# Last layer of a four-layer graph network: source blocks in pairs, count rows on four row groups, clamps shared by two engines in a fixed order

## Chip, cores and metric

One core of a Trainium2 chip runs one program. The metric is the device time of one execution in microseconds (us); the median of three runs is given. The core has five engines with a queue each, which they work through in order: TensorE (PE in the profile; its weight loads are PEld), VectorE (DVE), ScalarE (ACT), GpSimd (POOL) and SyncE (SP, which issues most transfers). Matmuls write to PSUM, eight banks of 128 x 512 float32.

## The reference, cut to what matters

Four graph layers on 4096 nodes with 64 features and one 0/1 adjacency matrix (about 32 edges a row). Each layer is applied to the ReLU of the normalized x and added to x. The change is in the last layer, with a little in the layer before it:

```python
def _L2_gnn_ref(X, adj, W, b):
    deg = jnp.clip(jnp.sum(adj, axis=1, keepdims=True) + 1.0, 1.0, None)
    h_neigh = (adj @ X + X) / deg
    z = jnp.concatenate([X, h_neigh], axis=1) @ W + b
    out = jax.nn.relu(z)
    return out / jnp.maximum(jnp.linalg.norm(out, axis=1, keepdims=True), 1e-12)

def _L3_gnn_ref(input, adj, weight, bias):
    support = input @ weight
    mask = (adj != 0).astype(support.dtype)
    rank = jnp.cumsum(mask, axis=1)
    deg = rank[:, -1:]
    k = jnp.minimum(deg, 100.0)
    pos = rank - (deg - k)
    w = mask * jnp.where(pos > 0, 0.5 ** (k - pos), 0.0)
    return w @ support + bias
```

So in the last layer an edge of a node weighs one half to the power of the number of the node's edges with a higher index, and only the last 100 edges count.

## The kernel before

Nodes are cut into 32 blocks of 128 (NB = 32, P = 128) and into 8 groups of 512 (G = 512, four blocks each). The adjacency lies transposed in memory: rows are sources, columns are targets. An earlier stage has written it to scratch memory as 8-bit masks (mask_d), whose byte is 1.0 in the fp8 format where there is an edge.

**Layer 2** (`layers_fast`, L2690 to L2738) runs over two halves of 2048 targets. For each half TensorE adds up all source blocks (nacc, L2701) and the edge counts (dc, L2711), and `layer2_group` (L2641) then finishes four groups, one after the other: fold (pnf, L2647), concatenation (cat, L2652 and L2653), two transposes, product with the weights (pz, L2658), ReLU and norm (zt and nrm, L2662 to L2671), addition to x (L2673), normalization (`norm_steps`, L964), and the support of the last layer (psup, L2681), split into a high and a low half in SS (L2684 to L2687). At the end of a half a matmul with a triangular matrix turns the counts of each source block into the counts of all later blocks (plate, L2737), and VectorE clamps them into the tile late (L2738): 128 rows are 4 groups of targets times 32 source blocks.

**The last layer** (L2741 to L2811) goes over four quarters u of 1024 targets (two groups of 512, NK = 2), and in each over the 32 source blocks j:

1. two count matmuls (L2767) with 32 contraction rows each: they pick the row of block j from late and write minus 128 times the number of edges in later blocks to every row of pv. They use the 32 rows that belong to the group of targets, so the two lie in different row groups of TensorE;
2. two edge matmuls (L2775) add, with the matrix tri, 100 x 128 for an edge of the row itself and minus 128 for each edge in a later row of the block. pv is two banks wide, and there are two of them;
3. ScalarE clamps pv at zero and writes 16-bit integers (L2784). Read as bfloat16, they are powers of two: the weights;
4. two adding matmuls (L2749) of the block before add up support times weights in sacc, two banks.

After 32 blocks ScalarE and VectorE copy sacc to ev (L2794), 16 small matmuls fold the high and the low half (pn, L2799), VectorE adds bias and x (L2807 and L2808), and GpSimd issues the transfer to the output (L2809).

VectorE has one more task: it checks that all entries of the adjacency are 0 or 1 (`count_odd`, L951 to L957; another program branch would otherwise compute the result). Each of 64 checks loads 1 MB of the float32 matrix (raw, two buffers) and takes one VectorE instruction. Sixteen of them belong to the last layer, none of them before the last support is ready (`issue_after(valued[-1].ins)`). The results are reduced after the layer (L2843 to L2846).

The order on each engine is set by a scheduler that builds the program; it may move an instruction ahead of others that were written earlier. Where code stands in `in_order` (L927), the instructions of TensorE, VectorE and ScalarE written there keep their order among themselves; others may come in between. Before the change the last layer isn't in such a block. A tile of a pool has as many buffers as `bufs` says, and an instruction that writes a buffer waits for the readers of its former content.

Of the kernel before, what the change touches and what calls it, by code (L numbers as in the profile page):

```python
# [24 lines left out]
P = 128  # L25
N = 4096
NB = N // P
D = 64
G = 512
NG = N // G  # L30
GB = G // P
# [804 lines left out]
def kernel(  # L836
# [111 lines left out]

        return col.unsqueeze(2).to_broadcast([P, col.shape[1], width])

    def count_odd(pool, c):  # L951

        raw = pool.tile([P, HW], F32, name="raw", tag="raw", bufs=2)
        nc.sync.dma_start(raw, adjT[c % NB * P : (c % NB + 1) * P, c // NB * HW : (c // NB + 1) * HW])
        nc.vector.scalar_tensor_tensor(  # L955
            raw, raw, 0.0, raw, ALU.is_gt, ALU.not_equal, accum_out=bad[:, c : c + 1]
        )  # L957
# [1576 lines left out]
    def layers_fast(es, wide, *sums):  # L2534
# [75 lines left out]
        with not_before_nodes():  # L2610
# [28 lines left out]
        late = lp.tile([P, 2, G], BF16, name="late")  # L2639

        def layer2_group(b0, part, deg):  # L2641

            bs = slice(b0, b0 + GB)
            hg = h[:, bs, :]
            pn = ps.tile([P, GB, D], F32, name="pnf", tag="misc")
            for b in range(GB):
                nc.tensor.matmul(  # L2647
                    pn[:, b, :], lhsT=part[:, b * P : (b + 1) * P], rhs=fold_h, start=True, stop=True
                )
            cat = work.tile([P, GB, 2 * D], F32, name="cat", tag="cat")  # L2650
            nc.gpsimd.tensor_copy(cat[:, :, 0:D], hg)
            nc.vector.scalar_tensor_tensor(cat[:, :, D:], pn, 1.0 / VALH, hg, ALU.mult, ALU.add)  # L2652
            nc.vector.tensor_tensor(cat[:, :, D:], cat[:, :, D:], over(deg, D), ALU.mult)  # L2653
            cT = work.tile([P, G], F32, name="cT", tag="cT")
            transpose_to(cT, [cat[:, b, :] for b in range(GB)], P, ps, nc.scalar.copy)
            pz = ps.tile([P, GB, D], F32, name="pz", tag="misc")
            for b in range(GB):
                nc.tensor.matmul(  # L2658
                    pz[:, b, :], lhsT=cT[:, b * P : (b + 1) * P], rhs=w2, start=True, stop=True
                )  # L2660
            zt = work.tile([P, GB, D], F32, name="zt", tag="zt")
            nc.vector.tensor_tensor(zt, pz, b2t.unsqueeze(1).to_broadcast([P, GB, D]), ALU.add)  # L2662
# [24 lines left out]
            nc.scalar.activation(SS[:, bs, 1, :], lo, AF.Copy, scale=LO)  # L2687


        with tc.tile_pool(name="ps_nacc", bufs=6, space=PSUM) as ps_acc:  # L2690
            for hf in range(2):
# [44 lines left out]
                pl = ps.tile([P, G], F32, name="plate", tag="misc")  # L2736
                nc.tensor.matmul(pl, lhsT=lat, rhs=cnt16[:, hf], start=True, stop=True)  # L2737
                nc.vector.tensor_scalar(late[:, hf], pl, VBITS, None, ALU.min)  # L2738


        ps_acc = es.enter_context(tc.tile_pool(name="ps_sacc", bufs=2, space=PSUM))  # L2741
        ps_v = es.enter_context(tc.tile_pool(name="ps_v", bufs=2, space=PSUM))
        for u in range(4):
            hs = slice((u % 2) * HO2, (u % 2 + 1) * HO2)
            accs = [ps_acc.tile([P, G], F32, name="sacc", tag="sacc") for _ in range(NK)]

            def add_up(j, w):
                for k in range(NK):
                    nc.tensor.matmul(  # L2749
                        accs[k],  # L2750
                        lhsT=SS[:, j].rearrange("p s d -> p (s d)"),
                        rhs=w[:, k * G : (k + 1) * G].bitcast(BF16),
                        start=(j == 0),
                        stop=(j == NB - 1),
                    )

            last = None
            for q in range(NQ):
                m = work.tile([P, JT, HO2], U8, name="m3", tag="m3", bufs=3)
                nc.sync.dma_start(m, mask_d[q][u // 2][:, :, hs])  # L2760
                for t in range(JT):
                    j = q * JT + t

                    pv = ps_v.tile([P, HO2], F32, name="pv", tag="pv")
                    for k in range(NK):
                        r = ((u % 2) * NK + k) * O
                        nc.tensor.matmul(  # L2767
                            pv[:, k * G : (k + 1) * G],
                            lhsT=blk[r : r + O, j, :],
                            rhs=late[r : r + O, u // 2, :],  # L2770
                            start=True,
                            stop=False,
                        )
                    for k in range(NK):
                        nc.tensor.matmul(  # L2775
                            pv[:, k * G : (k + 1) * G],
                            lhsT=tri,
                            rhs=m[:, t, k * G : (k + 1) * G].bitcast(F8),
                            start=False,
                            stop=True,  # L2780
                        )

                    w = work.tile([P, HO2], I16, name="w3b", tag="w3b", bufs=3)
                    nc.scalar.activation(w, pv, AF.Relu)  # L2784
                    if j % 8 == 4:
                        with tc.issue_after(valued[-1].ins):
                            count_odd(work, next(todo))
                    if last is not None:
                        add_up(*last)
                    last = (j, w)  # L2790
            add_up(*last)
            ev = work.tile([P, NK, G], F32, name="ev3", tag="ev3")
            for k in range(NK):
                (nc.vector.tensor_copy if k % 2 else nc.scalar.copy)(ev[:, k, :], accs[k])  # L2794
            for k in range(NK):
                b0 = (u * NK + k) * GB
                pn = ps.tile([P, GB, D], F32, name="pn3", tag="misc")
                for b in range(GB):
                    nc.tensor.matmul(  # L2799
                        pn[:, b, :],  # L2800
                        lhsT=ev[:, k, b * P : (b + 1) * P],
                        rhs=fold_3,
                        start=True,
                        stop=True,
                    )
                og = work.tile([P, GB, D], F32, name="og", tag="og")
                nc.vector.tensor_tensor(og, pn, b3t.unsqueeze(1).to_broadcast([P, GB, D]), ALU.add)  # L2807
                nc.vector.tensor_tensor(og, og, x[:, b0 : b0 + GB, :], ALU.add)  # L2808
                nc.gpsimd.dma_start(  # L2809
                    out[b0 * P : (b0 + GB) * P, :].rearrange("(b p) f -> p b f", p=P), og  # L2810
                )  # L2811
        assert next(todo, None) is None

    with tc.If(general == 0):
        with ExitStack() as es:
# [86 lines left out]
```

## Time and profile before

| | us |
|---|---|
| median of three runs (2017.6, 2022.05, 2024.63) | 2022.05 |
| the profiled execution | 2025.07 |
| its span, from the first to the last instruction | 2023.3 |
| TensorE matmul busy | 1805.3 (89%) |
| VectorE busy | 1539.6 (76%) |
| ScalarE busy | 1469.6 (73%) |
| GpSimd busy | 83.4 (4%) |
| first count matmul of the last layer, from the start of the span | 1811.7 |
| first edge matmul of its second quarter | 1880.2 |
| end of its last adding matmul | 2012.3 |

The profile is of one execution. A group's row gives line, engine, operation, output and inputs with shapes, the number of instructions, then busy time in us, the mean of one in ns, and the idle time of the engine just before them with what ended it. In the timeline a row gives start and length in us of instructions of one kind that follow each other; starts are counted from the start of the span. "L2775" is a line of the kernel before. Matmuls overlap: a 512-column matmul lasts 0.38 us in the rows, and the next one can start 0.22 us after it.

### The profile page before, as it was taken

What the parts mean: (1) busy time and instruction counts of PE and PEld (TensorE: products, weight loads), DVE (VectorE), ACT (ScalarE), POOL (GpSimd) and SP (SyncE); (2) the same over time, 40 slices, a digit from 0 to 9 for tenths busy, and PEclk for the clock granted to TensorE, in tenths of its full rate; (3) what the DMA queues carried; (4) which work ended last, traced back from release to release, by engine and by line L of the source; (5) the groups of instructions that cost most, each with busy time, mean ns of one, the idle gap of its engine ahead of it and who ended that gap; (6) DMA issues with size and microseconds to landing.
All of it is one profiled execution on the core that took longest, in us unless ns stands there. A gap on an engine that the chain in (4) does not pass through costs nothing. (4 is left out here: it accounts for less than half of the span.)

```text
span 2023.3 us, 44172 instructions
## 1 busy us (share of the span) xinstructions
PE 1805.3 (89%) x19323; PEld 816.2 (40%) x19340; DVE 1539.6 (76%) x2251; ACT 1469.6 (73%) x1427; POOL 83.4 (4%) x125
## 2 busy tenths in 40 slices
PE   5889999999999999997699958999999985889997
PEld 3444444444444444444244432333333333454332
DVE  5779988998789979996788768888878788533530
ACT  3768888899688878993889756777777743227676
POOL 2000100100000000001011000000000000000000
PEclk8989999999999999997799968999999997889999
DMA  8946565434211111103355415444344336312852
GB/s 111 179 116 101 100 101 72 166 123 161 96 49 49 49 49 54 54 2 93 127 178 181 154 59 188 141 145 155 121 144 150 116 119 221 125 63 74 290 188 65
DMA packets 117016, 239.05 MB, mean 118 GB/s; under 512 B 11062, under 2 KB 84006, under 8 KB 102054
## 3 DMA queue, kind: packets, MB, share of 16 engines
q1 hardware_dynamic: 101996, 192.95, 28.2%
q0 software_dynamic: 14816, 43.18, 12.0%
q8 instruction: 153, 2.51, 0.5%
q14 instruction: 51, 0.42, 0.1%
HBM read 245.37 MB, written 49.46 MB: 146 GB/s over the span
## 5 line engine op out<-in xcount | busy, mean ns | idle before, releaser
L1205 ACT ACTIVATE st<-srow,nt 128x2048 int8<-128x2048 f32 x352 | 682.6, 1994 | 84.6 <-DVE B L1211 83.7
L1211 DVE TENSOR_TENSOR B<-st,mres 128x1024 int32<-128x1024 int32 x256 | 311.8, 1220 | 64.7 <-PE accC L1541 39.8
L1541 PE MATMUL accB<-B,ybh 128*32 128x512 fp8e4 x3072 | 327.3, 384 | 13.0 <-DVE B L1211 13.0
L1541 PE MATMUL accD<-B,ybh 128*32 128x512 fp8e4 x2048 | 289.3, 387 | 1.6 <-DVE h L1674 1.6
L1541 PEld LDWEIGHTS <-ybh 128*32 128x32 bf16 (+1 forms) x6656 | 193.1, 98 | 213.3 <-issue 48.4
L1541 PE MATMUL accC<-B,ycn 128*32 128x512 fp8e4 x2272 | 267.9, 383 | 1.2 <-issue 1.2
L1541 PE MATMUL accC<-mres,ych 128*32 128x512 fp8e4 x2272 | 268.8, 384 | 0.0
L1541 PE MATMUL accL<-B,ybh 128*32 128x512 fp8e4 x1536 | 213.2, 386 | 3.4 <-DVE h L1673 3.4
L1541 PEld LDWEIGHTS <-ych 128*32 128x32 f16 x4096 | 164.5, 98 | 116.7 <-issue 9.4
L1199 DVE TENSOR_SCALAR st<-srow,nt 128x2048 uint8<-128x2048 f32 x160 | 205.1, 1284 | 2.1
L2352 PE MATMUL accj<-sg,who 128*64 128x512 f32 (+1 forms) x512 | 196.4, 614 | 6.9 <-DVE sg L2345 6.4
L2352 PE MATMUL acci<-sg,who 128*64 128x512 f32 (+1 forms) x512 | 196.5, 614 | 0.0
L2308 ACT ACTIVATE yt<-pu,consts 128x512 f32<-128x512 f32 x144 | 98.6, 686 | 99.7 <-PE pu L2307 99.6
L955 DVE SCALAR_TENSOR_TENSOR raw<-raw 128x2048 f32<-128x2048 f32 x64 | 146.0, 2284 | 31.4 <-DMA raw<-in_adj_dram 31.4
L2297 ACT ACTIVATE sg<-pl,rb 128x512 f32<-128x512 f32 x256 | 160.7, 678 | 7.9 <-PE pl L2292 4.7
L2784 ACT ACTIVATE w3b<-pv 128x1024 int16<-128x1024 f32 x128 | 130.9, 1023 | 42.6 <-PE pv L2775 41.1
L1205 ACT ACTIVATE st<-srowo,nto 128x1024 int8<-128x1024 f32 x128 | 138.0, 1136 | 14.8 <-DVE B L1211 12.4
L1541 PE MATMUL accC<-C,ych 128*32 128x512 fp8e4 x1824 | 143.0, 385 | 2.1 <-DVE C L1219 2.1
L1219 DVE TENSOR_TENSOR C<-B,mres 128x1024 int32<-128x1024 int32 x114 | 139.6, 1225 | 3.8 <-PE accC L1541 0.6
L1541 PEld LDWEIGHTS <-ycn 128*32 128x32 f16 x2272 | 105.9, 98 | 65.0 <-issue 5.3
L2345 DVE SCALAR_TENSOR_TENSOR sg<-pf,sg 128x512 f32<-128x512 f32 x112 | 72.1, 685 | 38.6 <-PE pf L2342 38.6
L2286 PE MATMUL pl<-nm,noid 128*128 128x512 fp8e4 x256 | 82.3, 393 | 14.3 <-ACT sg L2297 13.4
(498 smaller groups left out, 2678.8 us busy)
## 6 DMA issues: line engine op xcount, KB each, us to landing
raw<-in_adj_dram SPq DMA_DIRECT2D x64, 1024.0 KB, 5.8
mo<-edges SPq DMA_DIRECT2D x32, 512.0 KB, 3.9
noedge<-nmo POOLq DMA_DIRECT2D x32, 512.0 KB, 3.8
nm<-noedge SPq DMA_DIRECT2D x64, 256.0 KB, 3.1
m<-edges SPq DMA_DIRECT2D x16, 1024.0 KB, 4.7
m<-edges SPq DMA_DIRECT2D x32, 512.0 KB, 4.1
srow<-srow_d SPq DMA_DIRECT2D x15, 1024.0 KB, 6.8
mres<-in_adj_dram POOLq DMA_DIRECT2D x8, 1024.0 KB, 36.0
```

What stands on the lines that cost most here:

```text
L955: nc.vector.scalar_tensor_tensor(raw, raw, 0.0, raw, ALU.is_gt, ALU.not_equal, accum_out=bad[:, c : c + 1])
L1199: nc.vector.tensor_scalar(st[:, i, :].bitcast(U8), srow, negs[:, i : i + 1], EDGE, ALU.is_gt, ALU.mult)
L1205: nc.scalar.activation(st[:, i, :], srow, AF.Sign, bias=negs[:, i : i + 1], scale=-1.0)
L1211: nc.vector.tensor_tensor(B.bitcast(I32), st.bitcast(I32), edges.bitcast(I32), ALU.bitwise_and)
L1219: nc.vector.tensor_tensor(C.bitcast(I32), B.bitcast(I32), edges.bitcast(I32), ALU.bitwise_xor)
L1541: ins = nc.tensor.matmul(acc[k * O : (k + 1) * O, :], lhsT=values, rhs=moving(k), start=start, stop=stop,)
L2286: nc.tensor.matmul(pl, lhsT=noid, rhs=nm[:, b, :].bitcast(F8), start=True, stop=False)
L2297: nc.scalar.activation(sg[:, b0 + k, :], pl, AF.Sigmoid, bias=rb[:, j : j + 1], scale=1.0)
L2308: nc.scalar.activation(far[gi, gj][:, b, :], pu, AF.Sigmoid, bias=nb_t, scale=2.0 * DIST_K / (DIST_S * DIST_S),)
L2345: nc.vector.scalar_tensor_tensor(v[:, t, :], pf, F_K3, v[:, t, :], ALU.add, ALU.mult)
L2352: nc.tensor.matmul(acc[r : r + n, :], lhsT=XQ[:, src, cols], rhs=w, start=start, stop=stop)
L2784: nc.scalar.activation(w, pv, AF.Relu)
```

## The change

The last layer goes over pairs of source blocks: n counts 64 pairs, 16 in each quarter.

- A pair has four pv tiles of one bank each (before: two blocks in flight, of two banks each). Its four count matmuls come first, then its four edge matmuls. The second block's count rows are read from late_x, a second copy of late with its upper and lower 64 rows exchanged, so that the four matmuls use four different row groups. VectorE writes late_x with two more instructions a half.
- The clamp is done in pieces of 512: VectorE takes the first group of both blocks, ScalarE the second. In every fourth pair (n % 4 == 2) ScalarE takes all four, and VectorE checks 1 MB of the adjacency instead. The load of the next check's rows is issued right after a check. The checks are no longer held back until the last support is ready, so four of the sixteen are in the first quarter.
- The adding matmuls (four) of the pair before follow. The folds of a quarter are deferred: the last adding matmuls of a quarter stand in the first pair of the next, the copies to ev behind them, and the fold matmuls and the output in the pair after that.
- Everything stands in `in_order`.
- The bias is added to x by GpSimd in layer 2, behind the normalization, so that one VectorE operation remains for the output; its transfer is issued by SP. The reduction of the check results stands ahead of the last adding matmuls. In the built program the two operations that follow it also stand ahead of the last copy to ev on VectorE, and GpSimd has two more library reloads, one ahead of the first bias addition and one ahead of the all-partition reduction.

Line numbers after the change are 7 to 33 higher: L2762 is the count matmul, L2770 the edge matmul, L2784 and L2786 the clamps of ScalarE and VectorE, L2794 the adding matmul, L2805 the copy to ev, L2814 the fold, L2821 the output addition, L962 the check.

```diff
+    def load_rows(pool, c):
         raw = pool.tile([P, HW], F32, name="raw", tag="raw", bufs=2)
         nc.sync.dma_start(raw, adjT[c % NB * P : (c % NB + 1) * P, c // NB * HW : (c // NB + 1) * HW])
+        return raw, c
+
+    def count_odd(pool, c):
+        check_rows(*load_rows(pool, c))
+
+    def check_rows(raw, c):
         nc.vector.scalar_tensor_tensor(
...
+            nc.gpsimd.tensor_tensor(xg, xg, b3t.unsqueeze(1).to_broadcast([P, GB, D]), ALU.add)
...
                 nc.vector.tensor_scalar(late[:, hf], pl, VBITS, None, ALU.min)
+                for lo, hi in ((slice(0, D), slice(D, P)), (slice(D, P), slice(0, D))):
+                    nc.vector.tensor_scalar(late_x[lo, hf], pl[hi], VBITS, None, ALU.min)
 
         ps_acc = es.enter_context(tc.tile_pool(name="ps_sacc", bufs=2, space=PSUM))
-        ps_v = es.enter_context(tc.tile_pool(name="ps_v", bufs=2, space=PSUM))
-        for u in range(4):
...
+        ps_v = es.enter_context(tc.tile_pool(name="ps_v", bufs=4, space=PSUM))
+        PAIRS = NB // 2
+        rows = load_rows(work, next(todo))
+        edges, accs, last, ready = None, {}, None, None
+        both = [(i, k) for i in range(2) for k in range(NK)]
+
+        def ranks(u, j0):
+            pvs = {ik: ps_v.tile([P, G], F32, name="pv", tag="pv") for ik in both}
+            for i, k in both:
+                r = ((u + i) % 2 * NK + k) * O
+                nc.tensor.matmul(
+                    pvs[i, k],
+                    lhsT=blk[r : r + O, j0 + i, :],
+                    rhs=(late, late_x)[i][r : r + O, u // 2, :],
+                    start=True,
+                    stop=False,
+                )
+            for i, k in both:
+                nc.tensor.matmul(
+                    pvs[i, k],
+                    lhsT=tri,
+                    rhs=edges[:, j0 % JT + i, k * G : (k + 1) * G].bitcast(F8),
+                    start=False,
+                    stop=True,
+                )
+            return pvs
+
+        def clamp(pvs, alone):
+            w = work.tile([P, 2, HO2], I16, name="w3b", tag="w3b")
+            for i, k in both:
+                wk = w[:, i, k * G : (k + 1) * G]
+                if k or alone:
+                    nc.scalar.activation(wk, pvs[i, k], AF.Relu)
+                else:
+                    nc.vector.tensor_scalar(wk, pvs[i, k], 0.0, None, ALU.max)
+            return w
+
+        def add_up(u, j0, w):
+            if j0 == 0:
+                accs[u] = [ps_acc.tile([P, G], F32, name="sacc", tag="sacc") for _ in range(NK)]
+            for i, j in enumerate(range(j0, j0 + 2)):
...
+            if j0 + 2 < NB:
+                return None
             ev = work.tile([P, NK, G], F32, name="ev3", tag="ev3")
-            for k in range(NK):
-                (nc.vector.tensor_copy if k % 2 else nc.scalar.copy)(ev[:, k, :], accs[k])
+            for k, acc in enumerate(accs.pop(u)):
+                (nc.vector.tensor_copy if k else nc.scalar.copy)(ev[:, k, :], acc)
+            return u, ev
+
+        def bring(u, ev):
             for k in range(NK):
...
-                nc.vector.tensor_tensor(og, pn, b3t.unsqueeze(1).to_broadcast([P, GB, D]), ALU.add)
-                nc.vector.tensor_tensor(og, og, x[:, b0 : b0 + GB, :], ALU.add)
-                nc.gpsimd.dma_start(
+                nc.vector.tensor_tensor(og, pn, x[:, b0 : b0 + GB, :], ALU.add)
+                nc.sync.dma_start(
...
+        with in_order():
+            for n in range(4 * PAIRS):
+                u, j0 = n // PAIRS, n % PAIRS * 2
+                if j0 % JT == 0:
+                    q, c = j0 // JT, u % 2 * HO2
+                    edges = work.tile([P, JT, HO2], U8, name="m3", tag="m3", bufs=3)
+                    nc.sync.dma_start(edges, mask_d[q][u // 2][:, :, c : c + HO2])
+                pvs = ranks(u, j0)
+                w = clamp(pvs, n % 4 == 2)
+                if n % 4 == 2:
+                    check_rows(*rows)
+                    rows = (next(todo, None),)
+                    if rows[0] is not None:
+                        rows = load_rows(work, rows[0])
+                done = add_up(*last) if last else None
+                if ready:
+                    bring(*ready)
+                ready, last = done, (u, j0, w)
+            nc.vector.tensor_reduce(bad[:, 0:1], bad, AX.X, ALU.add)
+            bring(*add_up(*last))
...
-        nc.vector.tensor_reduce(bad[:, 0:1], bad, AX.X, ALU.add)
         odd = spool.tile([P, 1], F32, name="odd")
```

More of the change, by code (lines that the diff above doesn't have):

```diff
@@ L949, in over @@
         return col.unsqueeze(2).to_broadcast([P, col.shape[1], width])
-    def count_odd(pool, c):
+    def load_rows(pool, c):
         raw = pool.tile([P, HW], F32, name="raw", tag="raw", bufs=2)
         nc.sync.dma_start(raw, adjT[c % NB * P : (c % NB + 1) * P, c // NB * HW : (c // NB + 1) * HW])
+        return raw, c
+    def count_odd(pool, c):
+        check_rows(*load_rows(pool, c))
+    def check_rows(raw, c):
         nc.vector.scalar_tensor_tensor(
@@ L2638, in layers_fast @@
             nc.vector.tensor_scalar(fold_3, fold_h, M3, 2.0**27 / VAL, ALU.mult, ALU.mult)
-        late = lp.tile([P, 2, G], BF16, name="late")
+        late, late_x = (lp.tile([P, 2, G], BF16, name=n) for n in ("late", "late_x"))
         def layer2_group(b0, part, deg):
@@ L2738, in layers_fast @@
                 nc.vector.tensor_scalar(late[:, hf], pl, VBITS, None, ALU.min)
+                for lo, hi in ((slice(0, D), slice(D, P)), (slice(D, P), slice(0, D))):
+                    nc.vector.tensor_scalar(late_x[lo, hf], pl[hi], VBITS, None, ALU.min)
         ps_acc = es.enter_context(tc.tile_pool(name="ps_sacc", bufs=2, space=PSUM))
-        ps_v = es.enter_context(tc.tile_pool(name="ps_v", bufs=2, space=PSUM))
-        for u in range(4):
-            hs = slice((u % 2) * HO2, (u % 2 + 1) * HO2)
-            accs = [ps_acc.tile([P, G], F32, name="sacc", tag="sacc") for _ in range(NK)]
-            def add_up(j, w):
+        ps_v = es.enter_context(tc.tile_pool(name="ps_v", bufs=4, space=PSUM))
@@ L2748, in add_up @@
                 for k in range(NK):
                     nc.tensor.matmul(
-                        accs[k],
+                        accs[u][k],
                         lhsT=SS[:, j].rearrange("p s d -> p (s d)"),
-                        rhs=w[:, k * G : (k + 1) * G].bitcast(BF16),
+                        rhs=w[:, i, k * G : (k + 1) * G].bitcast(BF16),
                         start=(j == 0),
@@ L2755, in add_up @@
                     )
[L2757 to L2764, printed above, removed]
-                    for k in range(NK):
[L2766 to L2791, printed above, removed]
+            if j0 + 2 < NB:
+                return None
             ev = work.tile([P, NK, G], F32, name="ev3", tag="ev3")
-            for k in range(NK):
-                (nc.vector.tensor_copy if k % 2 else nc.scalar.copy)(ev[:, k, :], accs[k])
+            for k, acc in enumerate(accs.pop(u)):
+                (nc.vector.tensor_copy if k else nc.scalar.copy)(ev[:, k, :], acc)
+            return u, ev
+        def bring(u, ev):
             for k in range(NK):
```

## Prediction, made before the changed kernel ran

> **What bounds it now.** I read the slices first: after 1810 us TensorE is at nine tenths or more in nearly every slice, ScalarE and VectorE are not. The table of windows then splits the last layer into the quarter that overlaps with the tail of layer 2 (1811.7 to 1880), the other three quarters, and the end. Columns: length, then busy time and count of PE, PEld, DVE, ACT, POOL, then granted clock, DMA share, GB/s.
>
> ```profile
> 1811.70:1880.00 68.30, 64.17 (x322) 29.73 (x328) 25.88 (x66) 46.38 (x70) 0.80 (x2) 0.93 0.21 64
> 1880.00:2012.30 132.30, 129.55 (x609) 43.76 (x618) 39.24 (x47) 98.64 (x99) 4.95 (x7) 1.00 0.58 200
> 2012.30:2023.30 11.00, 2.02 (x17) 1.86 (x16) 2.21 (x5) 0.43 (x1) 1.49 (x2) 0.68 0.10 32
> ```
>
> In the second row PE is busy 129.6 of 132.3 us, ACT 98.6. The timeline of PE shows one block there:
>
> ```profile
> 1904.31 0.39 PE L2767 MATMUL pv<-late,LDf 32*128 32x512 bf16 x2
> 1904.62 0.61 PE L2775 MATMUL pv<-m,tri 128*128 128x512 fp8e4 x2
> 1905.11 0.59 PE L2749 MATMUL sacc<-w3b,XAf 128*128 128x512 bf16 x2
> 1905.64 0.39 PE L2767 MATMUL pv<-late,LDf 32*128 32x512 bf16 x2
> ```
>
> Two count matmuls start 4 ns apart (they lie side by side in two row groups); 0.32 us later the edge matmuls (tri), 0.22 apart; then the adding ones, 0.215 apart; the last is followed 0.31 later by the next block. Eleven blocks from 1891.19 to 1905.63 give 1.313 us each: PE-bound. Leaving or entering the four-row-group form costs 0.10 (0.31 and 0.32 against 0.215).
>
> The first quarter is something else: 32 blocks at 1.313 would be 42 us and it takes 68. Its list of waits has
>
> ```profile
> DVE cat L2652 <- PE pnf L2647: 13.5, 4, 3.9
> DVE zt L2662 <- PE pz L2658: 13.0, 4, 4.5
> ```
>
> that is, four layer-2 groups running one after the other (their x is written at 1823.67, 1838.46, 1853.24, 1868.29: 14.8 us each), with VectorE waiting in them. The blocks 16 to 31 need these groups, so this chain sets the quarter, and what is put into VectorE's queue inside it can lengthen it.
>
> **Durations for the new pieces.**
>
> ```profile
> L955 DVE SCALAR_TENSOR_TENSOR raw<-raw 128x2048 f32<-128x2048 f32 x64 | 146.0, 2284 | 31.4 <-DMA raw<-in_adj_dram 31.4
> ...
> L2784 ACT ACTIVATE w3b<-pv 128x1024 int16<-128x1024 f32 x128 | 130.9, 1023 | 42.6 <-PE pv L2775 41.1
> ```
>
> ```profile
> 1801.65 1.28 DVE L2723 COPY ev<-nacc 128x512 f32<-128x512 f32 x2
> ```
>
> ```profile
> 1263.44 1.24 ACT L2297 ACTIVATE sg<-pl,rb 128x512 f32<-128x512 f32 x2
> ```
>
> A VectorE clamp of 512 to int16 is not in the trace. The late row (L2738, the same kind of operation from PSUM to bf16) takes 0.690 and the ev copy 0.682; two copies in a row take 1.28, so the second starts 0.60 after the first. I take 0.69 and 0.605; the ends 0.61 (L2522, from SBUF) and 0.693 (the longest L2345) change no sum below, PE being later. A ScalarE clamp of 512: ends 0.51 (half of 1.023) and 0.68 (L2297); I take 0.59, the ev copy's 0.585 being the nearest (PSUM to SBUF, no bias). Two L2297 in a row take 1.24, an overlap of 0.10, so 0.49 to the next. Hand-overs: tri start to clamp start 0.476 (0.49 for the first after the count matmuls), clamp end to PE 0.05.
>
> **Last three quarters.** Count from the start of a pair's first tri.
> - PE alone: tri 4 x 0.22 = 0.88, adding 3 x 0.215 + 0.31 = 0.955, four count matmuls 0.012 + 0.316: 2.16, against 2 x 1.313 = 2.63 now. The gain is one count phase per two blocks instead of two.
> - But a pair takes all four pv banks, so the next pair's count matmuls wait for its clamps. That wait is new, and all later matmuls stand behind it. Shared pair: VectorE 0.49 + 0.605 + 0.69 = 1.785; ScalarE starts 0.70, then 1.19, ends 1.78; plus 0.05 = 1.84, when PE has just finished adding (0.88 + 0.955). So it stays at 2.17. Pair of ScalarE alone: 0.49 + 3 x 0.49 + 0.59 = 2.55, PE 2.60, next tri 2.92.
> - The check (2.284 + 0.08) starts when VectorE is done with the pair before and ends 2.0 into the alone pair; VectorE is next needed at 3.4. Hidden, with 1.4 to spare. Its rows: 2 MB per four pairs (9.4 us) is 210 GB/s; the trace moved more (slices of 290 and 220 GB/s). If they came late, each us beyond 1.4 would go straight into the pair.
> - Output folds: 16 matmuls L2799, 2.0 each quarter, now in the pair after next; PE has no idle there, so 2.0 stays, three times.
>
> Now: from the first tri of the second quarter (1880.21) to the end of the last adding matmul (2012.32) 132.1. Then: 35 x 2.17 + 12 x 2.92 + 3 x 2.0 + 2.9 for the last pair (clamps 1.84, four adding matmuls 0.645 + 0.38) = 119.9. **−12.2.**
>
> The trace shows two row groups side by side, not four; if they ran two by two, PE would need 0.22 more in each of the 35 shared pairs: between 0 and +7.6. I take 0, as the two start 4 ns apart. The Trainium skill (TensorE: Matmul & The Clock Gate, Part 3) gives a measured 3.07-fold speed-up for four row groups at this size, not 4. By it four count matmuls take 1.30 times 0.217, an estimated 0.05 more than I have, and the sum would be 1.9 us worse.
>
> **First quarter.** The built order puts into VectorE's queue there four checks, 24 clamps and two half-height late copies. A check costs its 2.36 less what VectorE would have idled at that place. Pair 2's stands between nrm and its reciprocal (idle 0.4): +2.0. Pair 6's, behind two clamps (1.3), ahead of zt (idle 2.7): +1.0, and 0.6 more because the second clamp waits for its tri. Pair 10's, behind two clamps, ahead of cat (idle 3.9): about 0. Pair 14's between the reciprocal and h (no idle): +2.4. Together +6.0. Of the clamps 4 are in those sums; of the other 20 (12.1 us at 0.605) the shorter waits of the four groups (0.5 for ln_sq, 0.8 for ln_var, 0.9 for sq: 8.8 in all) can cover most: +3.3. In return the count matmuls stand ahead of pdeg and the transposes earlier in PE's queue, so the first group's zt comes 1.3 earlier; and at the end four adding matmuls stand behind the last group instead of seven, at 0.43 each:
>
> ```profile
> 1876.89 3.07 PE L2749 MATMUL sacc<-w3b,XAf 128*128 128x512 bf16 x7 [1.97 <-ACT XAf L2687]
> ```
>
> That is −1.3 too. 6.0 + 3.3 − 1.3 − 1.3 = **+6.7**. Bounds: +2 (the gaps take all clamps and pair 2's check) to +24 (nothing hidden: 4 x 2.36 + 24 x 0.605).
>
> The Trainium skill (TensorE: Matmul & The Clock Gate, Part 1) has a rule against the change here: TensorE idle for a window of about 3.4 us falls to half clock. The row above agrees as far as it goes (0.43 instead of 0.215 after 5 us with little work). Were each of the four checks to cause it, a window of half clock holds about 16 matmuls at 0.215 more, an estimated +3.4 each if none of it were covered, and the sum would be +7 instead of −7.
>
> **The end.** One og operation instead of two (the x additions end at 15.91; a single one would end at 2015.24): −0.7. The two POOL issues of 0.75 in series become two SP issues; the second need not queue: −0.6. Bounds 0 and −2. The bias addition moves to POOL (eight of 128x256; its copies of that size take 0.40), between the cat copies, which come 13 us apart: hidden; a library reload ahead of it (about 9.9 us at the start of the trace, POOL silent from 1.95 to 11.81) fits into that gap as well, and the copies are 13 us ahead of need. The second reload, ahead of the reduction, has 100 us. The reduction itself (0.22, 0.37, 0.15, 0.87 in all) now stands ahead of the last ev copy on VectorE but behind the last clamps, beside the four last adding matmuls: hidden with 0.3 to spare; uncovered +0.6. SP: the out issues stand ahead of row and mask loads; the next mask is needed five pairs later, no cost. **−1.3.**
>
> **Sum.** +6.7 − 12.2 − 1.3 = −6.8. The profiled execution took 2025.1 (span 2023.3), so 2018.3 there. It lies 3.0 above the median 2022.05 of the runs, whose range is 2017.6 to 2024.6; against the median the forecast is 2015.2. The rivals are counted from the median too. What can be told from no change is 0.3%, 6 us; the forecast is just beyond it.
>
> **Rivals.**
> 1. The checks hit the layer-2 chain in full (slower). Place: VectorE's queue in the first quarter. For: it is that quarter's bound, and in-order clamps wait there for PE, which waits for the chain. Against: VectorE is idle 42 of 68 us there. Price at the far end +24: 24 − 12.2 − 1.3 = +10.5, 2032.5. It decides the sign from a lengthening of 13.5, and passes 6 us from 19.6.
> 2. The row groups don't run four at a time, so the change doesn't do what it says: −6.8 + 7.6 = +0.8, 2022.9. For: no row with four. Against: the two.
> 3. The banks become the bound: ScalarE's piece costs 0.68 as L2297 does. Then an alone pair takes 3 x 0.095 + 0.09 = 0.38 more and a shared one 0.16: 12 x 0.38 + 35 x 0.16 = 10.2, total +3.4, 2025.5. For: four banks, no spare. Against: the 0.585 of the ev copy.
>
> **Chances.** Forecast 0.48 (its own range 2008 to 2018); rival 1 0.18; 2 0.12; 3 0.16; further beyond on either side 0.02 faster, 0.04 slower. So faster by over 0.3% 0.50, within 0.28 (2 and 3), slower 0.22. Range 2006 to 2029: the lower end is +2, −12.2, −2 and two of scatter, the upper end takes in 2 and 3 and part of 1.
>
> **What would show it.** PE: four L2762 matmuls within 20 ns. Pairs of 2.17 and, every fourth, 2.92 from tri to tri; more than 2.3 for shared ones speaks for rival 2 (PE never idle) or 3 (PE waits for ACT). The second quarter's first tri near 1886.9; beyond 1895 rival 1. No wait of VectorE for raw. I would be wrong if masks or rows arrive late, or if the granted clock falls below 1.00 after 1890.

## The result and the profile after

The changed kernel took 2022.59 us (median of 22 runs, 2017.25 to 2027.65), the kernel before, beside it, 2022.43 (22 runs, 2015.66 to 2038.12): ratio 1.0001, 95% interval 0.9986 to 1.0015. No change. The range held the time; the likeliest case, faster by 6.8 us, didn't come. The profiled execution took 2022.61 us, its span is 2020.9, its mean granted clock 0.937 (before 0.941).

The table of windows of the changed kernel, cut at the same three places (columns as in the prediction: length, busy time and count of PE, PEld, DVE, ACT, POOL, granted clock, DMA share, GB/s):

```profile
1811.70:1890.40 78.70, 65.38 (x310) 32.15 (x309) 45.08 (x94) 34.88 (x76) 3.70 (x6) 0.83 0.33 107
1890.40:2009.90 119.50, 117.49 (x630) 45.92 (x626) 78.32 (x108) 65.99 (x124) 0.38 (x1) 1.00 0.57 187
2009.90:2020.90 11.00, 1.82 (x16) 1.68 (x16) 0.94 (x3) 0.00 (x0) 0.00 (x0) 0.68 0.16 34
```

The second stretch became shorter (132.3 to 119.5) with PE as full as before; the first became longer (68.3 to 78.7), with PE busy no longer than before (65.4 against 64.2), VectorE 45 us instead of 26, and a lower clock (0.83 against 0.93). To compare the two executions I count from the start of the first half's late operation, 1809.20 before and 1805.88 after. What lies ahead of it is the same but for four bias additions on GpSimd; in the runs below it starts anywhere from 1798.9 to 1810.8.

| us | before | forecast | after | difference |
|---|---|---|---|---|
| late to the second quarter (1880.21; 1890.39) | 71.0 | +6.7 | 84.5 | +13.5 |
| to the end of the last adding matmul (2012.32; 2009.26) | 132.1 | -12.2 | 118.9 | -13.2 |
| to the end of the span | 10.9 | -1.3 | 11.6 | +0.7 |
| sum | 214.0 | -6.8 | 215.0 | +1.0 |

(1880.21 is the first tri of the second quarter's second block, not of its first, as the table of before and the prediction have it: PE had run ahead to 1871.67 for that one. It moves the border between the first two rows by one block, 1.3 us, and no sum.)

The timeline of PE in the second stretch, two pairs where VectorE and ScalarE share the clamps:

```profile
1940.96 0.39 PE L2762 MATMUL pv<-late,LDf 32*128 32x512 bf16 x2
1940.97 0.39 PE L2762 MATMUL pv<-late_x,LDf 32*128 32x512 bf16 x2
1941.29 1.04 PE L2770 MATMUL pv<-m,tri 128*128 128x512 fp8e4 x4
1942.16 1.03 PE L2794 MATMUL sacc<-w3b,XAf 128*128 128x512 bf16 x4
1943.12 0.39 PE L2762 MATMUL pv<-late,LDf 32*128 32x512 bf16 x2
1943.13 0.39 PE L2762 MATMUL pv<-late_x,LDf 32*128 32x512 bf16 x2
1943.45 1.04 PE L2770 MATMUL pv<-m,tri 128*128 128x512 fp8e4 x4
```

Four count matmuls start within 12 ns, the first tri follows 0.33 later, and from tri to tri it is 2.16 us; the pairs where ScalarE clamps alone take 2.90. The groups of the checks and of ScalarE's clamps, from the page:

```profile
L962 DVE SCALAR_TENSOR_TENSOR raw<-raw 128x2048 f32<-128x2048 f32 x64 | 146.0, 2282 | 3.6 <-DMA raw<-in_adj_dram 3.6
...
L2784 ACT ACTIVATE w3b<-pv 128x512 int16<-128x512 f32 x160 | 86.3, 598 | 70.8 <-PE pv L2770 32.8
```

A check lasts what it lasted, and nearly nothing waits for its rows (3.6 us instead of 31.4). A ScalarE piece takes 0.598. The list of VectorE's waits in the first quarter:

```profile
DVE zt L2669 <- PE pz L2665: 11.0, 3, 4.6
DVE lo L2693 <- ACT XAf L2691: 5.8, 2, 4.0
...
DVE cat L2659 <- PE pnf L2654: 1.3, 2, 1.1
```

The waits for pz (13.0 before) are hardly shorter, those for pnf nearly gone (13.5 before). So VectorE did its new work partly in waits and partly in the way of the chain. The third group shows the worst place. Timeline of all engines around the fourth check (some rows left out):

```profile
1860.52 0.18 DVE L992 RECIPROCAL ln_var<-ln_var 128x4 f32<-128x4 f32 x1
1860.61 2.26 DVE L962 SCALAR_TENSOR_TENSOR raw<-raw 128x2048 f32<-128x2048 f32 x1
1862.80 0.08 DVE L962 DVE_READ_ACCUMULATOR raw<-raw 128x1 f32 x1
1862.80 0.42 DVE L993 SCALAR_TENSOR_TENSOR h<-h,ln_var 128x256 f32<-128x256 f32 x1
...
1863.37 0.74 PE L1007 MATMUL tr<-ident,h 128*64 128x128 f32 x4 [3.81 <-DVE h L993]
1864.14 0.58 ACT L1008 COPY hT<-tr 64x512 f32<-64x512 f32 x1 [3.66 <-PE tr L1007]
...
1864.78 1.97 PE L2688 MATMUL psup<-w3f,hT 64*128 64x64 f32 x8 [0.67 <-ACT hT L1008]
```

The check stands between the reciprocal and h, which had everything it needs. PE's next instruction is a transpose of h, so PE waits 3.8 us, and from 1863.69 the granted clock is 0.5: psup's eight matmuls take 1.97.

### The profile page after: what moved, and what is told of

It reads as the page before. It is cut to its first block, busy times and chain, and to the rows that moved or that the text cites. A ratio compares the mean times of both kernels' runs of the same rounds, so it can differ in the third digit from the quotient of the medians.

```text
span 2020.9 us, 44288 instructions
## 1 busy us (share of the span) xinstructions
PE 1793.3 (89%) x19340; PEld 820.6 (41%) x19340; DVE 1599.2 (79%) x2343; ACT 1425.0 (71%) x1459; POOL 83.3 (4%) x125
## 5 line engine op out<-in xcount | busy, mean ns | idle before, releaser
L962 DVE SCALAR_TENSOR_TENSOR raw<-raw 128x2048 f32<-128x2048 f32 x64 | 146.0, 2282 | 3.6 <-DMA raw<-in_adj_dram 3.6
L1212 ACT ACTIVATE st<-srowo,nto 128x1024 int8<-128x1024 f32 x128 | 138.0, 1137 | 15.3 <-DVE B L1218 12.9
L2784 ACT ACTIVATE w3b<-pv 128x512 int16<-128x512 f32 x160 | 86.3, 598 | 70.8 <-PE pv L2770 32.8
L2293 PE MATMUL pl<-nm,noid 128*128 128x512 fp8e4 x256 | 82.3, 393 | 13.7 <-ACT sg L2304 12.8
```

What stands on the lines that cost most here:

```text
L962: nc.vector.scalar_tensor_tensor(raw, raw, 0.0, raw, ALU.is_gt, ALU.not_equal, accum_out=bad[:, c : c + 1])
L1212: nc.scalar.activation(st[:, i, :], srow, AF.Sign, bias=negs[:, i : i + 1], scale=-1.0)
L2293: nc.tensor.matmul(pl, lhsT=noid, rhs=nm[:, b, :].bitcast(F8), start=True, stop=False)
L2784: nc.scalar.activation(wk, pvs[i, k], AF.Relu)
```

## The experiments

Stage times are of one profiled execution of each kernel, counted as in the table (first quarter / last three / end). Where two kernels have the same instructions in a stage they still differ: the changed kernel's first quarter took 84.5 in one run and 87.1 in another (out_on_pool below, same order there), its end 9.6 to 12.9.

**1. Without the first quarter's checks** (their columns of bad are set to zero by GpSimd):

```diff
                 if n % 4 == 2:
-                    check_rows(*rows)
+                    if n < PAIRS:
+                        nc.gpsimd.memset(bad[:, rows[1] : rows[1] + 1], 0.0)
+                    else:
+                        check_rows(*rows)
```

> The four checks of the first quarter are left out (their rows are still loaded, their results set to zero); all else as in the change. Measured is the first quarter, from the start of VectorE's late operation to the first edge matmul of the second quarter: 71.0 us in the kernel before, 84.5 in the changed one. Theory (the checks stand in VectorE's queue within the layer-2 chain and, by leaving TensorE idle, bring half clock): 74 to 77, and fewer than 25 us of half clock in it instead of 34. Rival (the clamps in a fixed order tie the chain to the pairs, the checks matter little): 81 or more.

68.1 / 118.3 / 12.1; 2004.82 us in all, 2024.27 for the kernel before beside it. The four checks cost 16.4 us of the first quarter, more than either case had; of half clock 13.8 us are left in it. VectorE's clamps are still there: by themselves they cost nothing, since h is ready every 14.7 us (18.32, 33.0, 47.7, 62.4 after late), as before the change (14.8). The fourth group's bursts on PE in this kernel:

```profile
1853.73 1.10 PE L2688 MATMUL psup<-w3f,hT 64*128 64x64 f32 x8
1854.76 1.10 PE L2654 MATMUL pnf<-fold_h,ev 128*128 128x64 f32 x8
```

**2. ScalarE alone clamps in the first quarter, the checks stay written where they are:**

```diff
-                w = clamp(pvs, n % 4 == 2)
+                w = clamp(pvs, n < PAIRS or n % 4 == 2)
```

> In the first quarter ScalarE clamps all pairs alone; the four checks stay. Theory (checks): 81 to 84 us for the first quarter, little gained. Rival (VectorE's clamps): 74 to 77.

68.0 / 119.7 / 9.6; 2004.68 us. Both expectations fell, because the kernel is not what I took it for: with no clamps of VectorE ahead of them, the scheduler moved the four checks up to 1675.9 to 1689.9, where layer 2 only begins (its first nacc matmul starts at 1686.2). The first quarter has none. It says the same as the first run, with a complete computation.

**3. No checks in the first quarter, sixteen in every third pair of the others:**

```diff
-                w = clamp(pvs, n % 4 == 2)
-                if n % 4 == 2:
+                check = n >= PAIRS and n % 3 == 0
+                w = clamp(pvs, n < PAIRS or check)
+                if check:
```

> In the first quarter ScalarE clamps alone and no check is made; the sixteen checks are in every third pair of the other three quarters. Both theories: the first quarter falls back to 71 to 73 us. The other three have 16 alone pairs instead of 12, each 2.90 instead of 2.16: 118.9 + 4 x 0.73 = 121.8. End 11.6. Together about 9 us (0.4%) less than the kernel before, ratio 0.995 to 0.997.

68.5 / 120.0 / 11.7; median 2004.45 us, ratio 0.9913 (0.9895 to 0.993). Four alone pairs more cost about 1 us, where 2.9 were expected (one of them, pair 33, hides behind a fold: 3.89 from tri to tri, as without it); the first quarter gives back 16, as in the first run, where 11.5 to 13.5 were expected.

**4. Count matmuls on two row groups only:**

```diff
-                r = ((u + i) % 2 * NK + k) * O
+                r = (u % 2 * NK + k) * O
-                    rhs=(late, late_x)[i][r : r + O, u // 2, :],
+                    rhs=late[r : r + O, u // 2, :],
```

> The second block's count matmuls read late instead of its exchanged copy, so the four count matmuls of a pair use two row groups, not four. If four row groups are what the pair gains by: shared pairs go from 2.16 to 2.38 us, alone ones stay near 2.90, and the last three quarters take 118.9 + 35 x 0.22 = 126.5. If the four banks hold the pair anyway: no change, 119.

89.0 / 127.4 / 12.9. The last three quarters lose 8.5 of the 13.2. The timeline of PE shows where: the four count matmuls now take 0.54 until the first tri, and a shared pair 2.37. That is 7.3 in 35 pairs; most of the rest is the second quarter's first pair, 3.85 instead of 2.44. (In the first quarter the scheduler ordered this kernel otherwise, so its 89.0 says nothing of the row groups.)

```profile
1952.13 0.60 PE L2762 MATMUL pv<-late,LDf 32*128 32x512 bf16 x4
1952.67 1.04 PE L2770 MATMUL pv<-m,tri 128*128 128x512 fp8e4 x4
1953.54 1.03 PE L2794 MATMUL sacc<-w3b,XAf 128*128 128x512 bf16 x4
1954.50 0.60 PE L2762 MATMUL pv<-late,LDf 32*128 32x512 bf16 x4
```

**5 and 6. The checks at other places in VectorE's order.** In both ScalarE alone clamps in the first quarter (as in run 2), and each of its four checks is held behind an instruction of layer 2. In run 5 it is the support's low half:

```diff
+                    with tc.issue_after(valued[min(3 + n // 4, 7)].ins):
                         check_rows(*rows)
```

> A complete computation. In the first quarter ScalarE alone clamps, and the four checks are held behind layer 2's instructions, so that they can't be moved ahead of it; in VectorE's order each now stands between the degree product of cat and the addition to pz (the first one ahead of cat). From the late operation to the first tri matmul of the second quarter the changed kernel took 84.5 us, and 68.0 with no check there. Theory (a check costs what sticks out of the wait that it lies in: between cat's end and zt's start VectorE has 2.6 us to wait for PE, ScalarE and PE again, a check is 2.28): 68 to 71. Rival (a check costs its 2.28 us wherever it stands, and the half clock with it): 77 to 84.

80.0 / 118.6 / 12.5. By the numbers the rival, but three of the four checks weren't where the text puts them. The first stands ahead of both operations on cat, the fourth behind them; the timeline of VectorE shows the second (the third is alike) between the two, one place earlier:

```profile
1831.83 0.42 DVE L2659 SCALAR_TENSOR_TENSOR cat<-pnf,h 128x256 f32<-128x256 f32 x1 [0.20 <-PE pnf L2654]
1832.17 2.28 DVE L962 SCALAR_TENSOR_TENSOR raw<-raw 128x2048 f32<-128x2048 f32 x1
1834.38 0.08 DVE L962 DVE_READ_ACCUMULATOR raw<-raw 128x1 f32 x1
1834.38 0.42 DVE L2660 TENSOR_TENSOR cat<-cat,degf 128x256 f32<-128x256 f32 x1
```

There nothing covers it: the next cat operation would have started at once. In run 6 each check is held behind that operation instead, which `scaled` collects:

```diff
+                    with tc.issue_after(scaled[min(4 + n // 4, 7)].ins):
                         check_rows(*rows)
```

> A complete computation. As the run with the held checks, with each of the first quarter's four checks one place later in VectorE's order: behind the degree product of cat, ahead of the addition to pz, where VectorE has 2.6 us to wait for PE, ScalarE and PE again, and a check is 2.28. In the held run the check stood ahead of that product and the chain waited 2.1 us for it in each group (first quarter 80.0). Theory (a check costs only what sticks out of the wait that it lies in): first quarter 68 to 70.5. Rival (it costs by its length in VectorE's queue, wherever it stands): 78 to 82.

68.7 / 119.8 / 12.2; 2003.99 us. Four checks in the first quarter, and no time for them:

```profile
1824.09 0.42 DVE L2661 TENSOR_TENSOR cat<-cat,degf 128x256 f32<-128x256 f32 x1
1824.43 2.28 DVE L962 SCALAR_TENSOR_TENSOR raw<-raw 128x2048 f32<-128x2048 f32 x1
1826.64 0.08 DVE L962 DVE_READ_ACCUMULATOR raw<-raw 128x1 f32 x1
1827.31 0.42 DVE L2671 TENSOR_TENSOR zt<-pz,b2f 128x256 f32<-128x256 f32 x1 [0.59 <-PE pz L2667]
```

VectorE ends the check and still waits 0.59 for pz. With four checks in the chain's waits the quarter takes 68.7, with none 68.0 (run 2): the clean test that run 5 was to be, and it decides for the theory. Between runs 5 and 6 lie 11.3 us, but not all of it is one place in the queue: in the second and third group, where the check stands just one place apart, the chain waits 2.1 us for it each time. The first group lost 2.5 with the check ahead of cat. The fourth lost 1.5 and the stretch behind its h 2.3, both with half clock in them, of which run 6 has almost none there.

**7. PE kept from idling, first try:** twelve matmuls that nobody reads behind pair 13's tri.

```diff
+                if n == 13:
+                    spin = ps.tile([P, G], F32, name="spin", tag="misc")
+                    for _ in range(12):
+                        nc.tensor.matmul(spin, lhsT=tri, rhs=edges[:, 0, 0:G].bitcast(F8), start=True, stop=True)
```

> A complete computation with twelve matmuls more, whose product nobody reads: they stand behind the tri matmuls of pair 13, where PE idled for 4.2 us in the changed kernel while VectorE was at the fourth check, after which the granted clock was 0.5 for 13.6 us. Theory (the half clock is what makes the fourth group so long: its matmul bursts psup, pnf, the transposes and pz took 3.1 us longer than with no check, and more behind them): no 0.5 between the third h and the fourth, the fourth group 19.4 -> 15.5 to 16.5 us, the first quarter 84.5 -> 80 to 81.5. Rival (the fourth group is long by its order, clamps and checks in the queues): 84 to 85, or longer by the added 2.6 us.

89.0 / 118.6 / 12.1, but no test of the two expectations: the tile shares its buffers with layer 2's, so the matmuls came at 1882.8, behind plate, long after the wait. The trace tells something else. The pairs stand behind these matmuls, so the fourth group ran with no pair's matmul and no clamp in it (of its PE rows the first two are left out), at a granted clock of 0.5 from 1861.69 on, 0.4 behind the third h:

```profile
1864.82 1.97 PE L2654 MATMUL pnf<-fold_h,ev 128*128 128x64 f32 x8
1867.85 1.08 PE L1007 MATMUL tr<-ident,cat 128*128 128x128 f32 x4 [1.07 <-DVE cat L2660]
1869.61 1.97 PE L2665 MATMUL pz<-w2f,cT 128*128 128x64 f32 x8 [0.68 <-ACT cT L1008]
1878.21 1.03 PE L1007 MATMUL tr<-ident,h 128*64 128x128 f32 x4 [6.62 <-DVE h L993]
```

From the third h to the fourth it took 16.8 us. Run 1, with pairs and clamps at full clock, took 14.7 there; the changed kernel, with the same slow bursts and with pairs and clamps, 19.4. So half clock alone doesn't make the fourth group's 19.4: 2.6 of it come from the pairs' matmuls and the clamps that stand between.

**8. Second try:** fourteen matmuls that add zero to an open sum (GpSimd clears the tile zero beforehand).

```diff
+                if n == 13:
+                    for _ in range(14):
+                        nc.tensor.matmul(accs[0][0], lhsT=zero, rhs=edges[:, 0, 0:G].bitcast(F8), start=False, stop=False)
```

> A complete computation with fourteen matmuls more, which add a zero product to an open sum: on PE they stand behind pair 13's tri matmuls and ahead of the transposes of h, where PE idled for 3.82 us in the changed kernel while VectorE did the fourth check; the order is otherwise the same. Fourteen by 0.216 us fill 3.0 of it. Theory (the half clock makes the fourth group's matmul bursts 3.1 us longer): no 0.5 between the third and the fourth h, the fourth group 19.4 -> 16 to 16.5 us, the first quarter 84.5 -> 81 to 82. Rival (the order of the queues makes it, not the clock): the fourth group 19 to 19.5, the first quarter 84 to 85.

82.3 / 119.5 / 11.6; the fourth group took 18.3 us: between the two expectations. The timeline of PE:

```profile
1862.70 3.19 PE L2838 MATMUL sacc<-m,zero 128*128 128x512 fp8e4 x14
1866.68 0.60 PE L1007 MATMUL tr<-ident,h 128*64 128x128 f32 x4 [0.79 <-DVE h L993]
1867.95 1.10 PE L2690 MATMUL psup<-w3f,hT 64*128 64x64 f32 x8 [0.67 <-ACT hT L1008]
1868.98 1.10 PE L2656 MATMUL pnf<-fold_h,ev 128*128 128x64 f32 x8
1870.42 0.61 PE L2796 MATMUL sacc<-w3b,XAf 128*128 128x512 bf16 x2 [0.34 <-ACT XAf L2696]
1871.15 1.09 PE L1007 MATMUL tr<-ident,cat 128*128 128x128 f32 x4
```

The wait is filled, psup and pnf run at full clock (1.10 each instead of 1.97), and the clock falls all the same, at 1871.12, 4.6 us behind the third h instead of 0.5. In this run, then, filling the long wait put the fall off by 4 us and didn't prevent it. (1.6 of the quarter's 2.2 us lie in the first group, where the half clock that the stage begins with ended earlier, and have nothing to do with the added matmuls.) How much of the fourth group's 19.4 us is the clock can't be read from this run alone, and the quarter's 2.2 us are no more than the 2.6 by which two equal first quarters differ (84.5 and 87.1).

**9. The fourth check moved to pair 16:**

```diff
-                w = clamp(pvs, n % 4 == 2)
-                if n % 4 == 2:
-                    check_rows(*rows)
+                check = n % 4 == 2 and n != 14 or n == 16
+                w = clamp(pvs, check)
+                if check:
+                    with tc.issue_after(valued[7 if n == 16 else 0].ins):
+                        check_rows(*rows)
```

> A complete computation: the first quarter's fourth check (pair 14) is done in pair 16 instead, in the second quarter, where ScalarE clamps alone then. Theory (the fourth check itself 1.9 us, and the half clock that follows PE's wait for it 3 to 5): first quarter 84.5 -> 77 to 79.5, last three quarters 118.9 -> 119.6 (one alone pair more). Rival (each check a quarter of the 16.4 us, no clock in it): 80 to 81.

80.7 / 119.3 / 12.2: the rival's number. The third group took 16.7 instead of 18.8 us (the check itself), the fourth still 18.2 instead of 14.7, and the clock fell to 0.5 for 10.2 us early in it, though PE's longest wait in the 3.4 us before was 0.85 (the end of one of 1.75). So the number is the rival's, but not its "no clock in it".

**10. The output from GpSimd's queue as before:**

```diff
-                nc.sync.dma_start(
+                nc.gpsimd.dma_start(
                     out[b0 * P : (b0 + GB) * P, :].rearrange("(b p) f -> p b f", p=P), og
```

> The changed kernel with the outputs issued by GpSimd's queue as before, on SP they land 3.0 us after their issue. In the runs with SP's queue the stretch from the last og operation to the end of the span was 6.7 to 9.6 us, in the kernel before (GpSimd's) 7.35. Theory (SP's queue lands the last output later and costs about 1 us of the end): 6.5 to 7.7, last landing near 2.2 us. Rival (the end's length is the scatter of what follows the landing, whichever the queue): 8 to 9.6.

87.1 / 119.1 / 9.7; from the last og to the end 6.82.

**11. The checks in 48 pieces, none in the first quarter:**

```diff
+    def check_part(raw, c, part):
+        lo, hi = (0, 683, 1366, HW)[part : part + 2]
...
-                w = clamp(pvs, n % 4 == 2)
+                w = clamp(pvs, n < PAIRS)
...
+                if n >= PAIRS:
+                    check_part(*rows, (n - PAIRS) % 3)
```

> A complete computation. ScalarE and VectorE clamp in turn in the first quarter's pairs by ScalarE alone (no check there); the sixteen checks are cut into three pieces of 683 columns, one behind VectorE's two clamps in each of the other 48 pairs, and no pair there is clamped by ScalarE alone. VectorE then has in a pair 1.29 us of clamps and a piece of about 0.8 (2.28 / 3), 2.09 of the 2.16 us that a shared pair lasts. Theory (a piece fits): all pairs 2.16, last three quarters 118.9 -> 110 to 112, first quarter 68 to 69, ratio to the kernel before 0.987 to 0.990. Rival (VectorE's turn sticks out by its handover, some 0.15 to 0.3 us a pair): 117 to 125, ratio 0.991 to 0.995.

68.5 / 111.1 / 10.2; median 1991.72 us, ratio 0.986 (0.9835 to 0.9885). (The text's "in turn" is a slip: in the first quarter ScalarE alone clamps.) Every pair is a shared one; the timeline:

```profile
1922.11 1.04 PE L2779 MATMUL pv<-m,tri 128*128 128x512 fp8e4 x4
...
1922.60 1.29 DVE L2795 TENSOR_SCALAR w3b<-pv 128x512 int16<-128x512 f32 x2
...
1923.80 0.86 DVE L965 SCALAR_TENSOR_TENSOR raw<-raw 128x682 f32<-128x682 f32 x1
...
1924.27 1.04 PE L2779 MATMUL pv<-m,tri 128*128 128x512 fp8e4 x4
...
1924.75 1.29 DVE L2795 TENSOR_SCALAR w3b<-pv 128x512 int16<-128x512 f32 x2
```

A piece takes 0.86, not 0.80, and still ends (1924.66) before the next clamp can start (0.48 after the tri). 2.16 from tri to tri: PE is the bound.

**12. Run 11 with the output on GpSimd's queue:**

> A complete computation: the run with the checks cut in pieces (1991.72 us, ratio 0.986, end 10.19 us, of it 7.27 behind the last og operation), its outputs issued by GpSimd's queue instead of SP's. Theory (GpSimd's queue lands the last output sooner): last og operation to the end of the span 6.6 to 7.4, end 9.3 to 10.1; the whole 1989 to 1992, ratio 0.984 to 0.987. Rival (the end's length is scatter, the queue decides nothing): last og to end anywhere in 6.7 to 10.

68.7 / 111.0 / 9.6, last og to the end 6.68; median 1995.70 us, ratio 0.9869 (0.9846 to 0.9893): not to be told from run 11. In the eleven profiled kernels that use SP's queue that last stretch was 6.7 to 10.0 us, median 9.2, nine of them 8.7 or more; in the three on GpSimd's 7.35, 6.82 and 6.68. GpSimd's is likely the shorter by about 2, but two SP runs are as short, and what in SP's end takes the time stays open.

## Why the prediction was right and wrong

The range held the time, in part by luck: the last three quarters gained what was forecast, the first quarter lost twice what was forecast, and the two cancelled. That the time lies beside rival 2's 2022.9 is chance: the row groups did run four at a time.

**Last three quarters, -12.2: right (-13.2).** Four row groups run side by side (run 4 takes 8.5 of the gain away: rival 2 falls with its price of 7.6 confirmed), the shared pair takes 2.16 (forecast 2.17), the alone pair 2.90 (2.92), ScalarE's piece 0.598 (0.59, so rival 3 falls), checks and rows are hidden. The rest is that a fold costs 1.73 and not 2.0.

**First quarter, +6.7: the wrong step, mis-sized by half (+13.5).** The bound it names, the layer-2 chain through VectorE's queue, is right: take the checks out of the chain and 16.4 us go (run 1), put them into its waits and 15.8 go (run 6). The pieces of the sum, from run 1 and the changed kernel side by side, operation by operation of the four groups:
- *Checks +6.0.* What the chain waits at the four places is 1.8, 1.5, 0.4 and 1.9 us, 5.6 in all (forecast 2.0, 1.6, 0, 2.4). Right.
- *The clock, 0 taken.* The prediction gave half clock a sentence and no term. (The sentence's 3.4 us a window is twice too much by its own row: at 0.43 a matmul, 3.41 us hold eight matmuls, not 16, so an estimated 1.7.) In the fourth group psup, pnf, the transposes and pz took 3.1 us longer at half clock, and from the last h to the second quarter it took 2.1 longer (psup 1.87 instead of 1.10 there). About 5, though not as the sentence has it, one window for each check: the clock fell twice after the start of the quarter, not four times, for 13.7 and 6.8 us. Run 8 shows psup and pnf at full clock, but not the whole price; in run 7 half clock with nothing between cost the fourth group 2.1 against run 1.
- *Clamps +3.3.* Wrong as an addition: without checks 0 (68.1 with VectorE's clamps, 68.0 without). With the checks in the queue, pairs and clamps are pushed into the chain's way on both engines: of the 16.4 us, 16.4 - 5.6 - 3.1 - 2.1 = 5.6 is left for that, by subtraction. Run 7's fourth group (16.8 with none of them in it, against 19.4) shows such a price; no run shows the 5.6 by itself. In run 5, with VectorE free of clamps, the quarter took 80.0, 4.5 less than 84.5, but its checks stand at other places. I added up prices of waits that each could be taken only once.
- *First group 1.3 earlier:* 0.1 (h at 18.3 without checks, 18.5 before). *Four adding matmuls instead of seven at the end, -1.3:* from the last h to the second quarter it took 8.1 before (1.3 of it by the border) and 5.7 in run 1; in the changed kernel 7.8, as the half clock took the gain back (adding matmuls at 0.42 apart again).

So rival 1 happened at a little over half its price. It put the turn of the sign at a lengthening of 13.5; that is what came, and the sum was zero.

**The end, -1.3: wrong sign (+0.7).** The og operation saved its 0.7 (last adding matmul to last og 2.92 instead of 3.58). Two issues on SP's queue instead of GpSimd's were to save 0.6; from the last og on it took 1.35 longer. Runs 10 and 12 point at the queue and not at the operation, within a scatter as large as the term. The 9.9 us that the prediction gives a library reload, by GpSimd's silence from 1.95 to 11.81, are in the profile a wait for a transfer (9.91 <-DMA ab); no row shows how long a reload takes. A bias addition took 0.73, not the 0.40 of a copy.

## What to carry to other kernels

Work put into the queue of an engine that "idles 42 of 68 us" costs what sticks out of the very wait that it is put into: look up the instruction behind it, and ask whether that one's inputs are ready. Here one place in the order, behind cat's product instead of ahead of it, was worth 2.1 us for each check, and moving all four into waits 11.3 with what followed from it (80.0 to 68.7); cutting the work into pieces that fit the gap of every pair saved another 8.7 of the other quarters (119.8 to 111.1). Idle time of one stage can be spent once: costs that each fit alone don't add up when they share the gaps, and where the chain was held up TensorE's clock fell too, which is part of the bill: in all seven kernels with checks in the chain's way it fell well inside the first quarter, in the six that have none there or have them in its waits not before the quarter's last 0.9 us.

## What the runs showed of the hardware

- The granted clock changes only at steps: in all runs its stretches of 0.5 inside the last layer last a multiple of 3.41 us (3.4, 6.8, 10.2, 13.7, 17.1, 23.9). The Trainium skill (TensorE: Matmul & The Clock Gate, Part 1) has a free-running window of 3413 ns, which agrees. Its condition, an idle window, doesn't: in run 8 PE was busy, by the profile, 2.74 us of the step ahead of the fall, with no gap over 0.34 in it. What does make it fall these runs don't settle.

```profile
1867.71:1871.12 3.41, 2.74 (x18) 2.04 (x18) 1.27 (x3) 0.97 (x3) 0.00 (x0) 1.00 1.05 399
1871.12:1874.53 3.41, 3.38 (x13) 2.07 (x13) 0.00 (x0) 0.59 (x1) 0.00 (x0) 0.50 0.09 36
```

- Four 32-row matmuls on four row groups cost PE no more than two: 0.33 us to the next matmul's start. Two by two they cost 0.54. The Trainium skill (TensorE: Matmul & The Clock Gate, Part 3) has 3.07-fold for four; by the starts here it is an estimated 4 x 0.217 / 0.33 = 2.6 with the change of form counted in, and no loss against two side by side (0.32 to the next start in the kernel before).
